# A feed-forward layer with quantised activations: one slot more in seven products, fewer quantisation passes, a head by 256 tokens

## The chip, the cores and the metric

The kernel runs on one core of one Trainium2 chip. The metric is the device time of one execution in microseconds (us). The engines are named as in the profile: PE (TensorE, matrix multiplication), DVE (VectorE), ACT (ScalarE), POOL (GpSimd) and SP (SyncE, which here only issues transfers). PE accumulates in PSUM banks; everything else lies in SBUF, the on-chip memory.

## What is computed

There are 4 batches of 1024 tokens with 512 features, a hidden width of 2048 and a condition of 128 numbers per batch.

```python
scale = cond @ norm_w.T + 1.0
ms = jnp.mean(x * x, axis=-1, keepdims=True)
h = x * (scale[:, None, :] * jax.lax.rsqrt(ms + EPS))
u = h @ up_w.T                              # 512 -> 2 * 2048
val, gate = jnp.split(u, 2, axis=-1)
h = val * jax.nn.gelu(gate, approximate=False)
hq = act_quant(h)      # per token: round(h * 127 / max|h|), then back
wq = weight_quant(down_w)   # ternary, one scale, mean|w|
y = hq @ wq.T + x
```

## The kernel before

**Tiling.** A batch is two halves of 512 tokens (`TOK`). The hidden width is 16 blocks `j` of 128 gate rows and 128 value rows. One block of one batch is a *slot* `g = b * 16 + j`. The float32 weights and activations are split into a high and a low float16 part, so that a product of two blocks needs six terms of two k-blocks each (`TERMS`).

**Plain slots and seven products.** In the first batch the slots `j < SEVEN` are plain: for each half, gate and value, 12 matmuls of 128x128 weights and 512 tokens (`plain_half`), 48 per slot. All other slots use a Strassen-Winograd form (`slot`): seven products of 6 matmuls (`product`), 42 per slot, on sums of weights and of tokens. The banks A, B and E collect them. Product 0 goes to A and is copied to B by ACT; product 4 goes to E and is copied to `v`; product 5 adds to A, and `first_value` keeps A for the second half's gate; product 1 adds to B, product 3 and 2 belong to the slot before, product 6 adds to A again, which gives the second half's value.

**Weights.** The first batch loads each block, scales it by a power of two, turns it (on PE through PSUM, or by a transposing transfer, `w_rows`), splits it and forms the sums. It spills them to DRAM; the later batches reload them through SP's queue (`s_load_x`, `s_load_y`; L909 transposing, L911 plain).

**Quantisation.** The largest |h| of each token is collected over pairs of slots (`pair_max`: a reduction L1275 and a merge L1277), spread by POOL over the partitions, and `token_scale` makes factors (L1296) and reciprocals of whole 128x128 tiles (L1302). `quant_scale` multiplies h (L1334); rounding adds and subtracts a large number, either in one DVE pass (`quant_round`, L1338) or in two ACT passes (`quant_up` L1342, `quant_down` L1346).

**Down.** The second matrix product of a batch is done one batch later, for 128 tokens `a` of both halves at a time, either plain (`down_mm`) or as a *pair* (`Pair`): seven products of 8 matmuls of 256 columns. The pairs of the last but one batch stand partly at the end, followed by the last batch's plain products.

**Order.** The code records its instructions, and a planner in the kernel (`Plan`, with costs and due times) sets the order of each engine's instructions. Each engine runs its own list strictly in that order and waits by semaphores.

**The head.** The condition gives the factors `scT` (products L690, power of two L706 to L738; for the other batches a 1536 wide multiplication L701 and sum L702). The first 512 tokens are loaded, squared and summed (L1480, L1482), scaled (L1487, L1489), turned by PE (L1494) and split into high and low parts (L1498, L1502). The first gate block is reduced (L786), scaled (L817), turned (L825) and split (L850, L859). Then PE multiplies (`plain_first`, L1199). Until then `keep_warm` gives PE matmuls without a use (L1510).

## Time and profile before

| what | before |
|---|---|
| median of 3 runs | 719.77 us (719.28 to 720.15) |
| span of the profiled execution | 717.4 us, so 2.4 us to the median lie around the span |
| PE busy | 711.5 us, 99% of the span |
| DVE busy | 605.2 us, 84% |
| ACT busy | 409.8 us, 57% |
| POOL busy | 130.0 us, 18% |
| first product | 14.36 us |
| transfers | 118.74 MB, 166 GB/s |

The span runs from the first to the last instruction on the core. A row of the timeline has start, length, engine, line, operation, out<-in and shape; what stands in brackets is the engine's idle time before it and what ended it. A row of the groups has the busy time of all instructions of a line and shape, the mean in ns, and the idle time before them. Matmuls are pipelined: one of 512 columns is given 0.379 us, while the next may start long before it ends. Engines that are not the bottleneck may be idle at no cost.

### The profile page before, as it was taken

How to read it: one execution, taken by the hardware profiler on the slowest of the kernel's cores; microseconds unless marked ns; L12 is line 12 of the kernel's file. 1: busy time of each engine (PE TensorE's matmuls, PEld its weight loads, DVE VectorE, ACT ScalarE, POOL GpSimd, SP SyncE). 2: the span in 40 equal slices, each digit the busy share in tenths (PEclk: the TensorE clock that was granted, in tenths of full speed). 3: DMA queues.
4: the chain of work that ended last, by engine and by line, in shares of the span. 5: the costliest groups of instructions: out<-in, count | busy, mean ns of one | idle time of the engine just before them, and what ended most of it. 6: DMA issues, size and time to landing. Idle time of an engine off the chain costs nothing.

```text
span 717.4 us, 10113 instructions
## 1 busy us (share of the span) xinstructions
PE 711.5 (99%) x3625; PEld 355.8 (50%) x3625; DVE 605.2 (84%) x903; ACT 409.8 (57%) x671; POOL 130.0 (18%) x138
## 2 busy tenths in 40 slices
PE   8999999999999999999999999999999999999998
PEld 4544444444444456664444445665444444445744
DVE  7978998899899899878899887767878888956897
ACT  5677688784546897553435786533333775332454
POOL 4753141020100004660023003700011000000000
PEclk9999999999999999999999999999999999999999
DMA  7778999999785896759234555778233444453414
GB/s 261 253 205 208 240 227 252 194 257 268 219 227 133 210 245 173 223 153 211 67 101 110 118 129 142 176 191 173 73 118 103 102 102 99 99 98 104 150 57 146
DMA packets 189134, 118.74 MB, mean 166 GB/s; under 512 B 151302, under 2 KB 158359, under 8 KB 189084
## 3 DMA queue, kind: packets, MB, share of 16 engines
q1 hardware_dynamic: 188794, 117.77, 64.3%
q8 instruction: 28, 0.46, 0.3%
q10 hardware_dynamic: 290, 0.33, 0.1%
q14 instruction: 22, 0.18, 0.1%
HBM read 59.20 MB, written 23.09 MB: 115 GB/s over the span
## 4 chain that ended last, share of the span: by engine, by line
PE 97%; DMA 1%; ACT 1%; POOL 0%; DVE 0%; issue 0%; SPq 0%; POOLq 0%
PE A L1141 40%; PE E L1141 20%; PE B L1141 10%; PE po L1413 9%; PE E L1156 6%; PE A L1156 4%; PE B L1156 3%; PE po L1362 2%; PE E L1362 1%; PE A L1362 1%; DMA H<-in_x_dram 1%; PE B L1413 1%; PE B L1362 0%; PE A L1199 0%; PE po L1494 0%; PE po L825 0%
## 5 line engine op out<-in xcount | busy, mean ns | idle before, releaser
L1141 PEld LDWEIGHTS <-SXY 128*128 128x128 f16 x2184 | 213.7, 98 | 250.9
L1141 PE MATMUL A<-R,SXY 128*128 128x512 f16 x1188 | 276.3, 379 | 0.0
L1141 PE MATMUL E<-R,SXY 128*128 128x512 f16 x594 | 145.3, 379 | 0.0
L1334 DVE TENSOR_TENSOR H<-H,am 128x1024 f32<-128x1024 f32 x64 | 76.6, 1222 | 0.2
L1141 PE MATMUL B<-R,SXY 128*128 128x512 f16 x312 | 76.6, 379 | 0.0
L1275 DVE TENSOR_REDUCE gm<-H 128x512 f32<-128x1024 f32 x56 | 69.0, 1232 | 0.9
L1252 ACT ACTIVATE t<-t,sg 128x512 f32<-128x512 f32 x55 | 39.7, 721 | 51.0 <-DVE t L1249 51.0
L1239 DVE SCALAR_TENSOR_TENSOR H<-A,sg,t 128x512 f32<-128x512 f32 x55 | 41.2, 749 | 31.9 <-PE A L1141 31.6
L1291 POOL PARTITION_ALL_REDUCE am<-R x8 | 15.5, 1934 | 288.4 <-DVE R L1277 288.4
L1236 ACT ACTIVATE t<-B,sg 128x512 f32<-128x512 f32 x55 | 37.8, 687 | 42.7 <-PE B L1141 42.6
L1227 ACT COPY B<-A 128x512 f32<-128x512 f32 x55 | 31.4, 571 | 53.3 <-PE A L1141 53.1
L1249 DVE TENSOR_TENSOR t<-E,t 128x512 f32<-128x512 f32 x55 | 37.9, 689 | 28.2 <-PE E L1141 27.7
L1413 PE MATMUL po<-wd,R 128*128 128x256 fp8e4 (+1 forms) x448 | 57.0, 275 | 0.0
L1219 ACT COPY t<-A 128x512 f32<-128x512 f32 x55 | 32.2, 585 | 43.4 <-PE A L1141 39.0
L1255 DVE TENSOR_TENSOR v<-A,v 128x512 f32<-128x512 f32 x55 | 37.9, 690 | 20.4 <-PE A L1141 19.6
L1413 PEld LDWEIGHTS <-R 128*128 128x128 bf16 (+1 forms) x480 | 47.0, 98 | 13.1
L1231 ACT COPY v<-E 128x512 f32<-128x512 f32 x55 | 32.2, 586 | 31.9 <-PE E L1141 15.6
L1342 ACT ACTIVATE H<-H 128x1024 f32<-128x1024 f32 x38 | 39.7, 1049 | 8.5 <-DVE H L1334 8.3
L1258 DVE SCALAR_TENSOR_TENSOR H<-v,sg,t 128x512 f32<-128x512 f32 x55 | 41.7, 759 | 1.7 <-ACT t L1252 1.4
L1156 PEld LDWEIGHTS <-SXY 128*128 128x128 f16 x264 | 25.8, 98 | 30.5
L1346 ACT ACTIVATE R<-H 128x1024 bf16<-128x1024 f32 x38 | 39.6, 1052 | 1.0 <-DVE H L1086 0.5
L1277 DVE TENSOR_TENSOR R<-R,gm 128x512 f32<-128x512 f32 x56 | 38.4, 686 | 0.9
(270 smaller groups left out, 919.2 us busy)
## 6 DMA issues: line engine op xcount, KB each, us to landing
SXY<-s_dram SPq DMA_DIRECT2D x57, 256.0 KB, 2.7
H<-in_L_cond_up_w_dram SPq DMA_DIRECT2D x13, 512.0 KB, 4.1
SXY<-s_dram SPq DMA_DIRECT2D x15, 384.0 KB, 3.7
xr<-in_x_dram SPq DMA_DIRECT2D x19, 256.0 KB, 2.9
out_dram<-xr SPq DMA_DIRECT2D x19, 256.0 KB, 2.1
s_dram<-SXY SPq DMA_DIRECT2D x12, 384.0 KB, 3.6
s_dram<-SXY SPq DMA_DIRECT2D x5, 896.0 KB, 6.7
H<-in_x_dram SPq DMA_DIRECT2D x8, 512.0 KB, 4.8
```

What stands on the lines that cost most here:

```text
L1141: PE.matmul(o, s[:, w, k, :], xs(l, k), start=start and n == 0, stop=stop and n == len(TERMS) - 1, skip_group_check=True,)
L1156: PE.matmul(ps, a[k // 2][:, w, k % 2, :], XP[:, l, k, h * TOK : (h + 1) * TOK], start=n == 0, stop=n == len(terms) - 1,)
L1239: DVE.scalar_tensor_tensor(h_half(g - 1, 0), prev["A"], gain(g - 1, 0), prev["t1"], ALU.mult, ALU.mult)
L1249: DVE.tensor_tensor(prev["t2"], prev["E"], prev["t2"], ALU.add)
L1252: ACT.activation(prev["t2"], prev["t2"], AF.Gelu, scale=gain(g - 1, 1))
L1258: DVE.scalar_tensor_tensor(h_half(g - 1, 1), prev["v"], gain(g - 1, 0), prev["t2"], ALU.mult, ALU.mult)
L1275: DVE.tensor_reduce(gm[0], v, AX.X, ALU.max, apply_absolute_value=True)
L1277: return [largest, lambda: DVE.tensor_tensor(m, m, gm[0], ALU.max)]
L1334: DVE.tensor_tensor(v, v, r.to_broadcast([P, 2, TOK]), ALU.mult)
L1342: ACT.activation(v, v, AF.Copy, bias=MAGIC)
L1346: ACT.activation(q, by_tile(v), AF.Copy, bias=-MAGIC)
L1413: PE.matmul(po, w[:, j], m, start=start and j == 0, stop=stop and j == n - 1, skip_group_check=True,)
```

## The change

1. `SEVEN` is 8 instead of 9: slot 8 goes by seven products.
2. The fourth pair of the last but one batch, at the end, is a `Pair` too; it was plain.
3. `Pair.first`: product B11 goes to one bank and ACT copies it to both halves of another one; before, its first matmul was 512 wide and wrote to both.
4. Block 2 is turned by a transfer (`w_rows(2)`) instead of by PE.
5. The head: the first 512 tokens are multiplied in two quarters of 256 (`plain_first`, `first_quarter`, `quarter_high`, `quarter_low`). Square sums and reciprocal roots come in two steps of 256 tokens. The first gate block is loaded ahead of x. The other batches' condition is loaded in the head, and its multiplication and sum stand there in DVE's order. `keep_warm` gives 20 matmuls instead of 23.
6. `first_value`: DVE writes `E = A + v`, and product 2 adds to it; before, ACT copied A out and DVE added it to E after product 2. The gelu reads E.
7. `quant_scale` writes int8 in place; one ACT copy makes bfloat16 of it.
8. Maxima over groups of 4 or 2 slots (`group_max`).
9. Reciprocals of the scales of the first three batches on a compact 32x32 tile (`token_rows`), by four small transfers; the last batch keeps `token_scale`.
10. Block maxima of the up weights come from ACT sums from block 3 on (was 6), two small operations go to POOL, and the sums of the first tokens' parts (`first_sums`) read PSUM.
11. The order is no longer planned in the kernel but read from a table (`ORDER`, a permutation of the recorded instructions).

```diff
-BY_SUM = 6
+BY_SUM = 3
-class Plan:
+class Book:
...
     def order(self):
-        steps = self.steps
...
+        packed = zlib.decompress(base64.b85decode("".join(ORDER)))
+        order, at = [], 0
+        for n in range(0, len(packed), 2):
+            at += int.from_bytes(packed[n : n + 2], "little", signed=True)
+            order.append(self.steps[at])
+            at += 1
...
-    SEVEN = 9
+    SEVEN = 8
...
     def plain_first(between):
...
+        parts = [(w, 0, k) for w in range(2) for k in range(NK)] + [(0, 1, k) for k in range(NK)]
+        order = [(t, q, *p) for t in (1, 0) for q in range(2) for p in parts[: 2 * NK]]
+        order += [(t, q, *p) for t in (1, 0) for q in range(2) for p in parts[2 * NK :]]
...
+            c = slice(q * TOK // 2, (q + 1) * TOK // 2)
             PE.matmul(
-                ps[t], a[:, w, k % 2, :], XP[:, l, k, :TOK],
-                start=w + l + k == 0, stop=l == 1 and k == NK - 1,
+                ps[t][:, c], a[:, w, k % 2, :], XP[:, l, k, c],
+                start=q + w + l + k == 0, stop=l == 1 and k == NK - 1,
...
         def first_value():
             product(5, g, cur["A"], False, True)
-            cur["t2"] = wpool.tile([P, TOK], F32, name=f"t2_{g}", tag="t2")
-            ACT.copy(cur["t2"], cur["A"])
+            DVE.tensor_tensor(cur["E"], cur["A"], cur["v"], ALU.add)
...
             product(2, g - 1, prev["E"], False, True)
-            DVE.tensor_tensor(prev["t2"], prev["E"], prev["t2"], ALU.add)
...
-            ACT.activation(prev["t2"], prev["t2"], AF.Gelu, scale=gain(g - 1, 1))
+            prev["t2"] = wpool.tile([P, TOK], F32, name=f"t2_{g}", tag="t2")
+            ACT.activation(prev["t2"], prev["E"], AF.Gelu, scale=gain(g - 1, 1))
...
-    def pair_max(b, i, h):
-        v = h_slots(b * NJ + 2 * i, 2)[:, :, h].rearrange("p j t -> p t j")
+    GROUPS = {0: (4, 4, 4, 2, 2), 1: (2, 4, 4, 4, 2), 2: (4, 4, 4, 2, 2), 3: (4, 2, 4, 4, 2)}
+    def group_max(b, j, h):
+        n = group_ends(b)[j]
+        v = h_slots(b * NJ + j - n + 1, n)[:, :, h].rearrange("p j t -> p t j")
...
+    def token_rows(b, am):
+        rows = sm.tile([NR, 2 * TOK // NR], F32, name=f"rows_{b}", tag="rows", bufs=1)
+        SP.dma_start(out=row_dram[b : b + 1], in_=am[0:1])
+        SP.dma_start(out=rows, in_=row_dram[b : b + 1].rearrange("o (r t) -> (o r) t", r=NR))
+        def invert():
+            DVE.tensor_scalar(rows, rows, 1e-5, 1.0 / 127.0, ALU.max, ALU.mult)
+            DVE.reciprocal(rows, rows)
+            SP.dma_start(out=am_dram[b : b + 1].rearrange("o (r t) -> (o r) t", r=NR), in_=rows)
+            SP.dma_start(out=am, in_=am_dram[b].partition_broadcast(P))
...
+    def whole(v):
+        return v.bitcast(I8)[:, :, :TOK]
     def quant_scale(b, i, h, s):
-        DVE.tensor_tensor(v, v, r.to_broadcast([P, 2, TOK]), ALU.mult)
+        DVE.tensor_tensor(whole(v), v, r.to_broadcast([P, 2, TOK]), ALU.mult)
-    def quant_round(b, i, h):
-        DVE.tensor_scalar(q, by_tile(v), MAGIC, MAGIC, ALU.add, ALU.subtract)
-    def quant_up(b, i, h):
-        ACT.activation(v, v, AF.Copy, bias=MAGIC)
-    def quant_down(b, i, h):
-        ACT.activation(q, by_tile(v), AF.Copy, bias=-MAGIC)
+    def quant_round(b, i, h, eng):
+        if eng is ACT:
+            ACT.copy(q, by_tile(whole(v)))
...
         def first(self, banks):
-            self.product(self.part(0, 0), "B11", k1, 1, True, True, True)
-            ACT.copy(k1[:, :HALF], k1[:, HALF:])
             self.product(self.s[1], "T1", k3, 0, True, True)
+            self.product(self.part(0, 0), "B11", k3, 1, True, True)
+            o = k3[:, HALF:].rearrange("p (y o) -> p y o", y=1).to_broadcast([P, 2, HALF])
+            ACT.copy(k1.rearrange("p (y o) -> p y o", y=2), o)
...
     first_load(0, 2)
+    w_load(0, (1,))
     first_load(2, 2)
-    w_load(0, (1,))
...
-    keep_warm(13)
-    first_sum(1)
+    keep_warm(WARM)            # WARM = 10
+    first_sum(1, DVE)
+    rsqrt(ssq0[:, 0:2], rs0[:, 0:2])
...
     def third_slot():
-        w_turn(2)
-        w_high(2)
-        w_low(2)
+        w_rows(2)
...
-    BY_VECTOR = {(0, 0), (0, 1), (1, 0), (4, 0), (6, 0), (7, 0), (7, 1)}
+    BY_VECTOR = set()
...
-    old = [pairs[a] for a in range(3)]
+    old = [pairs[a] for a in range(3)] + [Pair(b - 1, 3)]
```

**What the order does, place 1: DVE in the head.** In each row stand the line, the operation and its out<-in with the shape. `ssq` are the square sums of x, `wam` the largest values of a weight block, `rs` the reciprocal roots, `scT` the condition's factors, and the CAST makes the high part of the first gate block. Before, these rows lead to that CAST:

```order
L1482 SCALAR_TENSOR_TENSOR R,ssq_0_87<-H 128x512
L786 TENSOR_REDUCE wam_95<-H 128x1
L659 TENSOR_SCALAR wam_95<-wam_95 128x1
L793 TENSOR_SCALAR sw<-wam_95 128x1
L1489 TENSOR_SCALAR H<-H,rs_0_88 128x512
L796 RECIPROCAL iv_96<-sw 128x1
L786 TENSOR_REDUCE wam_102<-H 128x1
L659 TENSOR_SCALAR wam_102<-wam_102 128x1
L793 TENSOR_SCALAR sw<-wam_102 128x1
L737 TENSOR_SCALAR scT<-scT,ux 128x4
L796 RECIPROCAL iv_96<-sw 128x1
L850 CAST SXY<-E_100 128x2x256
```

Now the stretch from the first gate block's reduction begins with these rows, and another stretch follows with the wide reductions of blocks 1 and 2:

```order
L443 TENSOR_REDUCE wam_96<-H 128x1
L364 TENSOR_SCALAR scT<-scT 128x4
L359 TENSOR_TENSOR R<-R 128x1536
L1151 SCALAR_TENSOR_TENSOR R,ssq_0_88<-H 128x512
L366 TENSOR_REDUCE mx_92<-scT 128x1
L360 TENSOR_REDUCE scT<-R 128x3x4
L318 TENSOR_SCALAR wam_96<-wam_96 128x1
L1158 TENSOR_SCALAR H<-H,rs_0_89 128x512
L450 TENSOR_SCALAR sw<-wam_96 128x1
L1151 SCALAR_TENSOR_TENSOR R,ssq_0_88<-H 128x512
```

```order
L1158 TENSOR_SCALAR H<-H,rs_0_89 128x512
L450 TENSOR_SCALAR sw<-wam_103 128x1
L318 TENSOR_SCALAR d_0_94<-d_0_94 1x1
L453 RECIPROCAL iv_97<-sw 128x1
L383 TENSOR_SCALAR dg_95<-ident,d_0_94 1x1
L443 TENSOR_REDUCE wam_96<-H 128x2
L393 RECIPROCAL ux<-B_91 128x1
L396 COPY dx<-B_91 128x1
L395 TENSOR_SCALAR scT<-scT,ux 128x4
L443 TENSOR_REDUCE wam_103<-H 128x2
L505 CAST SXY<-E_101 128x2x256
```

The 1536 wide multiplication and sum and both wide block reductions have moved ahead of the CAST.

**Place 2: PE at the first product.** The turned blocks go to banks `po`, `A` and `E`, and the products to `B` and `A`. Before:

```order
L1494 MATMUL A_91<-ident,H 128x128
L825 MATMUL E_101<-ident,H 128x128
L1494 MATMUL A_91<-ident,H 128x128
L825 MATMUL E_101<-ident,H 128x128 x3
L1199 LDWEIGHTS SXY
L1199 MATMUL B_90<-R,SXY 128x512
```

And now, with a matmul of `keep_warm` (L1200) ahead of the first product:

```order
L1170 MATMUL po_100<-ident,H 128x128
L1170 MATMUL A_93<-ident,H 128x128
L1200 LDWEIGHTS H
L1200 MATMUL A_90<-H 128x512
L845 LDWEIGHTS SXY
L845 MATMUL B_91<-R,SXY 128x256
```

The first product now has 256 columns; all turning of the first tokens still stands ahead of it.

**Place 3: SP at the start of the second batch.** `SXY<-s_dram` are the reloads of spilled weights; `am` holds the scales on all partitions. Before:

```order
L909 DMA_TRANSPOSE SXY<-s_dram 128x4x128
L909 DMA_TRANSPOSE SXY<-s_dram 128x12x128
L945 DMA xn_111<-in_L_cond_down_w_dram 128x1024
L1310 DMA am_dram<-am_116 1x1024
L911 DMA SXY<-s_dram 128x1024
L911 DMA SXY<-s_dram 128x512
L945 DMA xt_112<-in_L_cond_down_w_dram 128x1024
```

And now:

```order
L975 DMA am_dram<-rows_127 32x32
L564 DMA_TRANSPOSE SXY<-s_dram 128x4x128
L564 DMA_TRANSPOSE SXY<-s_dram 128x12x128
L564 DMA_TRANSPOSE SXY<-s_dram 128x4x128
L976 DMA am_116<-am_dram 128x1024
L566 DMA SXY<-s_dram 128x512
L598 DMA xn_112<-in_L_cond_down_w_dram 128x1024
```

The write of the reciprocals and their broadcast now stand between reloads, and each must wait for what it moves.

696 lines of the change are left out of this document (217 added, 479 removed), and 14 rows, old and new, of tables (MENDS, MOVES).

## The prediction

> **What bounds the kernel now.** I read the share of each engine and the chain of waits first.
>
> ```profile
> span 717.4 us, 10113 instructions
> PE 711.5 (99%) x3625; PEld 355.8 (50%) x3625; DVE 605.2 (84%) x903; ACT 409.8 (57%) x671; POOL 130.0 (18%) x138
> PE 97%; DMA 1%; ACT 1%; POOL 0%; DVE 0%; issue 0%; SPq 0%; POOLq 0%
> ```
>
> TensorE (PE) is busy for 711.5 of 717.4 us and is 97% of the chain. Which part could shrink is seen in the busy time by stage (length, then busy PE, PE weight load, DVE, ACT, POOL, the granted clock, DMA share, GB/s):
>
> ```profile
> 0.00:14.36 14.36, 11.60 (x52) 5.86 (x53) 10.01 (x49) 6.20 (x13) 5.34 (x12) 1.00 0.77 247
> 14.36:20.64 6.28, 6.23 (x32) 3.14 (x32) 5.76 (x13) 5.66 (x15) 5.57 (x7) 1.00 0.95 327
> 60.00:714.40 654.40, 654.32 (x3348) 327.43 (x3346) 555.36 (x767) 369.09 (x592) 96.19 (x93) 1.00 0.64 160
> 714.40:717.40 3.00, 0.00 (x0) 0.00 (x0) 0.44 (x1) 0.00 (x0) 0.00 (x0) 1.00 0.44 152
> ```
>
> From 60 us to the end PE rests 0.08 us in 654. So the time is three things: a head until the first product at 14.36 us, PE's own work, and a 3 us tail. Work taken from DVE or ACT is worth nothing by itself there; a PE instruction taken out is worth its pitch, and a later first product costs what it is late. The pitches come from the timeline (start, length):
>
> ```profile
> 1.26 1.46 PE L1510 MATMUL A<-H 128*128 128x512 f16 x3 [1.26 <-DVE H L607]
> 3.37 2.31 PE L1510 MATMUL A<-H 128*128 128x512 f16 x5
> 5.69 0.65 PE L1510 MATMUL A<-H 128*128 128x512 f16 x2
> 7.17 2.98 PE L1510 MATMUL A<-H 128*128 128x512 f16 x13
> 18.25 1.04 PE L825 MATMUL po<-ident,H 128*128 128x128 f32 x8
> 20.64 2.75 PE L1156 MATMUL A<-R,SXY 128*128 128x512 f16 x12
> 660.18 1.04 PE L1413 MATMUL po<-wd,R 128*128 128x256 fp8e4 x8
> ```
>
> One matmul of 512 columns lasts 0.379, so twelve in 2.75 are (2.75-0.38)/11 = 0.216 apart. Eight of 256 columns, or eight float transposes, are (1.04-0.27)/7 = 0.109 apart.
>
> **The change on PE**, counted in the order of both kernels:
> - Slot 8 in seven products: 48 to 42 matmuls of 512, -6 x 0.216 = -1.30.
> - The fourth old pair as a Strassen pair: 32 x 512 becomes 56 x 256, 56 x 0.109 - 32 x 0.216 = -0.81.
> - `Pair.first` no longer sends B11 to two banks: one 512 becomes a 256 in eleven pairs, -11 x 0.107 = -1.18. ACT copies 512 columns instead of 256 there; a copy of 512 is 0.585 long (first row of the next fence), and ACT is free 43% of the span.
> - Block 2 turned by DMA: 8 transposes fewer, -8 x 0.109 = -0.87. SP gets one transposing transfer more.
> - One matmul more that sets a bank, +0.22; the head's 24 x 512 as 48 x 256, +0.05.
>
> Sum -3.89 us. That is the gain, if PE never waits where it did not wait before.
>
> **The change on DVE and ACT**, by the groups (busy us, mean ns, idle time before):
>
> ```profile
> L1219 ACT COPY t<-A 128x512 f32<-128x512 f32 x55 | 32.2, 585 | 43.4 <-PE A L1141 39.0
> L1255 DVE TENSOR_TENSOR v<-A,v 128x512 f32<-128x512 f32 x55 | 37.9, 690 | 20.4 <-PE A L1141 19.6
> L1277 DVE TENSOR_TENSOR R<-R,gm 128x512 f32<-128x512 f32 x56 | 38.4, 686 | 0.9
> L1302 DVE RECIPROCAL am<-am 128x128 f32<-128x128 f32 x32 | 27.9, 918 | 0.2
> L1334 DVE TENSOR_TENSOR H<-H,am 128x1024 f32<-128x1024 f32 x64 | 76.6, 1222 | 0.2
> L1338 DVE TENSOR_SCALAR R<-H 128x1024 bf16<-128x1024 f32 x26 | 18.0, 701 | 0.2
> L1342 ACT ACTIVATE H<-H 128x1024 f32<-128x1024 f32 x38 | 39.7, 1049 | 8.5 <-DVE H L1334 8.3
> ```
>
> DVE loses 26 roundings (18.0), 24 merges of maxima (24 x 0.686 = 16.5) and 24 reciprocals (24 x 0.918 = 22.0), some 56 us; ACT loses the 55 copies (32.2), and its 76 rounding passes become 64 (12 x 1.05 = 12.6). On the path all this is 0: PE waits for neither after 60 us. The price of a multiply that writes int8 is in no row: between 0.70 (the rounding's, with a narrow output) and twice 1.22. I take 1.22, its row now; even 64 x 1.22 = 78 us more would be 22 over the 56 saved, and the 16% that DVE is free are 112 us. The cover is gone only if a long instruction stands just ahead of one that PE needs. That place exists: `E = A + v` now stands on DVE between product 5 and product 6, which overwrites A; before, an ACT copy stood there. Product 2's six matmuls cover 1.30 us. The result needs 0.379-0.216 = 0.16 to arrive and the addition 0.69, so 0.44 is left. At worst a doubled maximum (about 2 x 1.23) has just started and PE waits 2 us; from nothing to 1.3 us over 55 slots, I take 0.2, near the lower end, since DVE stood idle 20 us before L1255 in the same position. The four small transfers of the compact scales stand on SP; they are a rival below.
>
> **The head** decides the rest.
>
> ```profile
> 6.03 0.63 ACT L1480 ACTIVATE H<-H 128x512 f32<-128x512 f32 x1 [3.25 <-DMA H<-in_x_dram]
> 7.76 0.69 DVE L1482 SCALAR_TENSOR_TENSOR R<-H 128x512 f32<-128x512 f32 x1 [0.26 <-DMA H<-in_x_dram]
> 8.42 0.69 DVE L786 TENSOR_REDUCE wam<-H 128x1 f32<-128x512 f32 x1
> 9.14 0.15 DVE L659 TENSOR_SCALAR wam<-wam 128x1 int32<-128x1 int32 x1
> 10.14 0.49 DVE L1489 TENSOR_SCALAR H<-H,rs 128x512 f32<-128x512 f32 x1 [0.66 <-POOL rs L1002]
> 10.54 0.16 DVE L796 RECIPROCAL iv<-sw 128x1 f32<-128x1 f32 x1
> 12.61 0.69 DVE L850 CAST SXY<-E 128x512 f16<-128x512 f32 x1 [0.67 <-PE E L825]
> 13.94 1.21 DVE L786 TENSOR_REDUCE wam<-H 128x2 f32<-128x1024 f32 x1
> 14.36 2.10 PE L1199 MATMUL B<-R,SXY 128*128 128x512 f16 x9 [0.37 <-ACT R L1498]
> 30.32 2.28 DVE L701 TENSOR_TENSOR R<-R 128x1536 f32<-128x1536 f32 x1
> 33.84 1.74 DVE L702 TENSOR_REDUCE scT<-R 128x12 f32<-128x1536 f32 x1
> ```
>
> The first x rows land at 6.0; the first product reads the gate weights that the CAST at 12.61 writes. In the order of the changed kernel DVE does far more before that CAST: the multiplication and sum of the other batches' scales, which now stand at 30 and 34 us, and the 1024 wide reductions of blocks 1 and 2, of which one now starts at 13.94. From DVE's first square sum (it waits for the first x rows) to the end of the CAST I count: two square sums 1.38, two scalings 0.98, one 512 wide reduction 0.69, the 1536 wide one 1.74, two 1024 wide ones 2.42, the CAST 0.69, fifteen small ones of some 0.15 = 2.25; together 10.15. Successive ones start some 0.08 before the last has ended (10.14+0.49 against 10.54), so nine long ones take 0.7 off: 9.4 us. The first gate block (256 KB) now goes ahead of x, and 192 KB of scales beside it: at 247 GB/s (the first window) 1.0 and up to 0.8 us, so x lands at 7.0 to 7.8. The CAST ends at 16.4 to 17.2. The first product then starts at 16.7 to 17.7, allowing up to 0.5 us for waits between; I take 17.2, 2.84 us later than now. That PE starts on 256 tokens instead of 512 helps only its other condition, the ACT pass at 14.36.
>
> Behind it, from 14.36 to 20.64 there are 24 x 0.216 + 8 x 0.109 = 6.05 us of PE work in 6.28, so 0.23 of waiting. Changed, the low gate part comes one 256 wide and one 512 wide DVE instruction behind the CAST (0.4, an estimate from half of 0.69, and 0.69), and six products of 0.109 cover 0.65 of that: 0.4 of waiting; the value weights' low parts come behind it in the same way, another 0.4. I take 0.8, with 0.3 and 1.6 (twice that) as ends. That is +0.57.
>
> Sum: -3.89 + 2.84 + 0.57 + 0.20 = -0.28 us. The span becomes 717.1. The median of the runs is 719.77, the profiled span 717.4, so 2.4 us lie around it: **719.5 us**. Its own range, from 16.7, 0.3 and 0 to 17.7, 1.6 and 1.3, is 718.3 to 721.9, most of it below 721.2. 0.2% of this time, about what the runs can tell from no change, is 1.44 us.
>
> [...] PE stands nearly idle for about 3 us ahead of that CAST, with fewer keep-warm matmuls (20, not 23). In the rows above, the matmuls at 3.37 are (2.31-0.38)/4 = 0.48 apart (0.43 in pairs) and those at 7.17 0.217, with the granted clock given as 1.00: PE was slow from its first matmul at 1.26 until between 5.69 and 7.17. If that state returned, it would last 4.4 to 5.9 us of products and cost half of it, 2.2 to 3.0 us.
> [...]
>
> **The rivals.**
> 1. *Faster: the head is not later.* DVE may reach the CAST as early as now if the long reductions run while it would wait for x anyway, and 256 tokens need half the turned columns. Then -3.89 + 0.2 + 0.2 = -3.5, 716.3 us. For it: DVE waits before 6.0 and 0.66 at 10.14. Against: 9.4 us of instructions behind x do not fit between 6.0 and 13.3. Chance 0.21, the cases between included.
> 2. *Slower: reloads just in time.* Each batch reloads spilled weights through SP's queue. They land (min, median, max us) in
>
> ```profile
> DMA to landing us min/median/max: 2.6/3.9/6.7
> DMA to landing us min/median/max: 2.2/2.8/5.9
> ```
>
> for the transposing ones (L909) and the plain ones (L911). In the changed order SP has, among them at each batch's start, the transfers of the scales, of which the broadcast waits for DVE's reciprocal, and some reloads stand only 18 to 28 matmuls (3.9 to 6.0 us) ahead of their first product. A landing of 6.7 then holds PE up by 0.7 to 2.8 us. Against: the median is below. From one such wait per later batch (3 x 0.7 = 2.1) it decides: 721.2 to 724, say 722. Chance 0.13.
> 3. *Slower: the slow clock*, as above: 719.5 + 2.6 = 722.1. Against: turning matmuls fall into the gap. Chance 0.10.
> 4. That the change does not do what it says would show in PE's count; the order excludes it.
>
> **How the numbers follow.** My forecast has 0.56, within 0.2% by its own range. Rival 1 gives faster 0.21; rivals 2 and 3 slower 0.23. About 0.1 of rival 1 lies below 717.0, and about 0.1 of the slower cases above 722.3, so that is the range.
>
> **What would show it.** Right: the CAST of the first gate block ends near 17 us, the first product (L845) starts at 16.7 to 17.7, PE's work is 3.9 us less, and no PE wait behind 25 us; DVE falls to some 550 us with no effect. Wrong: a first product before 15.5 (rival 1), PE waits for DMA at batch starts (2), pitches of 0.218 for 256 columns in the head (3), or PE waits for `E = A + v` summing to over 1.3 us.

## The result, and the profile after

The changed kernel takes 740.36 us (median of 4 runs) against 719.63 of the kernel before beside it, a ratio of 1.0283 [1.0263, 1.0303]: 2.8% slower, where 719.5 was forecast. The profiled execution has a span of 737.9 us, 20.5 more than before. The first lines of its page and the shares of the chain:

```profile
span 737.9 us, 10039 instructions
PE 714.2 (97%) x3657; PEld 360.1 (49%) x3657; DVE 570.8 (77%) x789; ACT 365.4 (50%) x622; POOL 142.7 (19%) x164
PE 70%; DVE 16%; issue 4%; POOL 2%; ACT 2%; DVEq 0%; ACTq 0%; POOLq 0%
```

DVE is busy 34 us less than before and stands 167 us idle, and yet it is now 16% of the chain, where it was 0%. The stages show where (length, then busy PE, PE weight load, DVE, ACT, POOL, granted clock, DMA share, GB/s):

```profile
0.00:20.13 20.13, 13.18 (x49) 7.08 (x49) 14.46 (x53) 5.72 (x13) 6.16 (x14) 0.83 0.73 231
81.00:100.00 19.00, 14.96 (x62) 6.18 (x61) 18.24 (x29) 11.78 (x22) 4.38 (x6) 0.91 0.78 208
100.00:734.60 634.60, 625.55 (x3236) 316.15 (x3233) 489.25 (x613) 296.70 (x486) 88.70 (x95) 1.00 0.61 155
```

From 100 us on PE rests 9 us in 635, between 81 and 100 another 4 (before, from 60 us on: 0.08 in 654). What PE waited for, summed by the instruction that ended the wait (us in total, times, longest):

```profile
PE E L802 <- DVE H L830: 3.7, 2, 3.0
PE A L787 <- DVE E L865: 3.6, 6, 0.9
PE A L373 <- DVE mx L366: 3.5, 1, 3.5
PE A L787 <- DVE v L901: 2.9, 4, 1.0
PE E L787 <- DVE E L865: 1.4, 2, 0.8
PE A L787 <- DVE H L885: 0.8, 1, 0.8
```

Nearly every wait behind the head is for DVE, at four different instructions (`E = A + v` is L865), none for a transfer. DVE's groups (busy us, mean ns, idle before) tell what is dear and what is not:

```profile
L1010 DVE TENSOR_TENSOR H<-H,am 128x1024 int8<-128x1024 f32 x64 | 76.4, 1224 | 0.9 <-DMA am<-am_dram 0.7
L932 DVE TENSOR_REDUCE gm<-H 128x512 f32<-128x2048 f32 x18 | 66.9, 3718 | 0.0
L927 DVE TENSOR_REDUCE R<-H 128x512 f32<-128x2048 f32 x6 | 22.3, 3716 | 0.0
L932 DVE TENSOR_REDUCE gm<-H 128x512 f32<-128x1024 f32 x14 | 17.2, 1231 | 0.2
```

The int8 multiply costs what the float32 one did (1.224). The maximum over 4 slots, 24 times, costs 3.72 us: three times that over 2 slots (1.23), not twice. One of the waits, in the timelines of DVE and of PE:

```profile
130.41 3.69 DVE L932 TENSOR_REDUCE gm<-H 128x512 f32<-128x2048 f32 x1
134.01 0.68 DVE L901 TENSOR_TENSOR v<-A,v 128x512 f32<-128x512 f32 x1
134.74 1.45 PE L787 MATMUL A<-wd,SXY 128*128 128x512 f16 x6 [0.95 <-DVE v L901]
```

The reduction waits for nobody; behind it stands the addition that must read bank A before PE may overwrite it. The five rows for L787 and L802 above are 15 waits; in 13 of them a 3.7 us reduction lies in the 5 us ahead.

The rest is in the head. DVE's rows:

```profile
7.77 1.75 DVE L359 TENSOR_TENSOR R<-R 128x1536 f32<-128x1536 f32 x1
9.44 0.68 DVE L1151 SCALAR_TENSOR_TENSOR R<-H 128x512 f32<-128x512 f32 x1
10.05 0.15 DVE L366 TENSOR_REDUCE mx<-scT 128x1 f32<-128x4 f32 x1
10.12 1.74 DVE L360 TENSOR_REDUCE scT<-R 128x12 f32<-128x1536 f32 x1
18.14 0.17 DVE L393 RECIPROCAL ux<-B 128x1 f32<-128x1 f32 x1 [2.02 <-PE B L389]
19.62 0.67 DVE L505 CAST SXY<-E 128x512 f16<-128x512 f32 x1
```

and those of ACT (the first x rows land) and PE (the power of two of the scale; keep-warm; the first product):

```profile
8.46 0.63 ACT L1149 ACTIVATE H<-H 128x512 f32<-128x512 f32 x1 [5.68 <-DMA H<-in_x_dram]
10.26 0.27 PE L373 MATMUL A<-ident,mx 128*1 128x128 f32 x1 [3.45 <-DVE mx L366]
14.78 1.91 PE L1200 MATMUL A<-H 128*128 128x512 f16 x4
20.35 0.50 PE L845 MATMUL B<-R,SXY 128*128 128x256 f16 x3 [0.19 <-DVE SXY L505]
```

x lands at 8.46 (6.03 before), DVE turns to it at 9.44, behind a 1536 wide multiplication, and the first product comes at 20.35 instead of 14.36. Behind the wait of 3.45 PE is slow: four matmuls in 1.91 are (1.91-0.63)/3 = 0.427 apart.

For the accounts I take the starts of all matmuls from the trace. The time from the first product to the last matmul is split into waits (what a matmul starts later than the usual distance of its kind, over 0.02 us) and work (the rest); behind the last matmul comes the tail. Before: 14.36 + 0.61 + 699.08 + 3.40 = 717.4. After: 20.35 + 18.83 + 695.24 + 3.51 = 737.9. So the head costs 6.0, the waits 18.2, the work is 3.84 less.

### The profile page after: what moved, and what is told of

It reads as the page before. It is cut to its first block, busy times and chain, and to the rows that moved or that the text cites. A ratio compares the mean times of both kernels' runs of the same rounds, so it can differ in the third digit from the quotient of the medians.

```text
span 737.9 us, 10039 instructions
## 1 busy us (share of the span) xinstructions
PE 714.2 (97%) x3657; PEld 360.1 (49%) x3657; DVE 570.8 (77%) x789; ACT 365.4 (50%) x622; POOL 142.7 (19%) x164
## 4 chain that ended last, share of the span: by engine, by line
PE 70%; DVE 16%; issue 4%; POOL 2%; ACT 2%; DVEq 0%; ACTq 0%; POOLq 0%
PE A L787 33%; PE E L787 16%; PE B L787 7%; PE po L1083 7%; DVE gm L932 5%; PE po L1033 2%; PE E L802 2%; DVE R L927 1%; DVE E L865 1%; DVE H L885 1%; PE E L1033 1%; DVE v L901 1%; PE B L1083 1%; PE A L1033 1%; DVE H L904 1%
## 5 line engine op out<-in xcount | busy, mean ns | idle before, releaser
L787 PEld LDWEIGHTS <-SXY 128*128 128x128 f16 x2184 | 213.6, 98 | 250.3 <-issue 11.3
L787 PE MATMUL A<-R,SXY 128*128 128x512 f16 x1188 | 290.3, 379 | 5.8 <-DVE E L865 3.0
L787 PE MATMUL E<-R,SXY 128*128 128x512 f16 x594 | 153.1, 379 | 0.8 <-DVE E L865 0.8
L932 DVE TENSOR_REDUCE gm<-H 128x512 f32<-128x2048 f32 (+1 forms) x32 | 84.1, 2630 | 0.3
L787 PE MATMUL B<-R,SXY 128*128 128x512 f16 x312 | 83.1, 379 | 0.0
L885 DVE SCALAR_TENSOR_TENSOR H<-A,sg,t 128x512 f32<-128x512 f32 x56 | 41.9, 748 | 48.1 <-PE A L787 39.1
L1010 DVE TENSOR_TENSOR H<-H,am 128x1024 int8<-128x1024 f32 x64 | 76.4, 1224 | 0.9 <-DMA am<-am_dram 0.7
L898 ACT ACTIVATE t<-E,sg 128x512 f32<-128x512 f32 x56 | 38.4, 688 | 71.7 <-PE E L787 71.7
L1015 ACT CAST R<-H 128x1024 bf16<-128x1024 int8 x64 | 65.4, 1044 | 15.3 <-DVE H L1010 14.7
L1083 PE MATMUL po<-wd,R 128*128 128x256 fp8e4 x448 | 66.1, 273 | 0.2 <-DVE R L1071 0.2
L901 DVE TENSOR_TENSOR v<-A,v 128x512 f32<-128x512 f32 x56 | 38.5, 688 | 27.8 <-PE A L787 27.7
L865 DVE TENSOR_TENSOR E<-A,v 128x512 f32<-128x512 f32 x56 | 39.0, 697 | 26.9 <-PE A L787 20.2
L802 PEld LDWEIGHTS <-SXY 128*128 128x128 f16 x264 | 26.1, 99 | 34.5 <-issue 6.0
L802 PE MATMUL E<-R,SXY 128*128 128x512 f16 x132 | 32.7, 392 | 3.0 <-DVE H L830 3.0
L1124 DVE SCALAR_TENSOR_TENSOR xr<-po,dq,xr 128x256 f32<-128x256 f32 (+1 forms) x36 | 21.4, 611 | 9.7 <-PE po L1083 6.6
```

The source lines that it names most:

```text
L787: PE.matmul(o, s[:, w, k, :], xs(l, k), start=start and n == 0, stop=stop and n == len(TERMS) - 1, skip_group_check=True,)
L802: PE.matmul(ps, a[k // 2][:, w, k % 2, :], XP[:, l, k, h * TOK : (h + 1) * TOK], start=n == 0, stop=n == len(terms) - 1,)
L865: DVE.tensor_tensor(cur["E"], cur["A"], cur["v"], ALU.add)
L885: DVE.scalar_tensor_tensor(h_half(g - 1, 0), prev["A"], gain(g - 1, 0), prev["t1"], ALU.mult, ALU.mult)
L898: ACT.activation(prev["t2"], prev["E"], AF.Gelu, scale=gain(g - 1, 1))
L901: DVE.tensor_tensor(cur["v"], cur["A"], cur["v"], ALU.add)
```

## Experiments

All runs stand in one table. e14 and e16 start from the kernel before, all others from the changed one. The columns are time and ratio to the kernel before (its medians were 719.4 to 719.7), start of the first product, waits behind it, and PE's work, in us.

| run | time | ratio | first product | waits | work |
|---|---|---|---|---|---|
| before | 719.63 | 1 | 14.36 | 0.61 | 699.08 |
| after | 740.36 | 1.0283 [1.0263, 1.0303] | 20.35 | 18.83 | 695.24 |
| e1_half | 722.62 | 1.0044 [1.0029, 1.0058] | 20.44 | 1.56 | 695.30 |
| e2_split | 742.23 | 1.0324 [1.0309, 1.0340] | 20.43 | 23.44 | 695.26 |
| e3_head | 746.98 | 1.0376 [1.0360, 1.0392] | 20.38 | 23.81 | 695.20 |
| e4_headsplit | 748.95 | 1.0406 [1.0391, 1.0422] | 19.76 | 28.50 | 695.21 |
| e5_twice | 722.04 | 1.0036 [1.0024, 1.0049] | 19.74 | 1.86 | 695.28 |
| e6_condhalf | 726.54 | 1.0101 [1.0086, 1.0116] | 18.32 | 7.23 | 695.26 |
| e7_head2half | 726.63 | 1.0098 [1.0083, 1.0113] | 16.21 | 10.01 | 695.24 |
| e8_forms | 728.13 | one run | 19.04 | 8.52 | 695.26 |
| e9_threes | 731.95 | 1.0173 [1.0158, 1.0188] | 19.52 | 11.07 | 695.28 |
| e10_head3threes | 738.43 | 1.0262 [1.0215, 1.0308] | 16.10 | 21.35 | 695.23 |
| e11_xfirst | 724.28 | 1.0067 [1.0052, 1.0082] | 22.57 | 1.35 | 695.28 |
| e12_scalefirst | 721.74 | 1.0033 [1.0021, 1.0045] | 19.99 | 1.91 | 695.26 |
| e13_scalewide | 724.74 | 1.0084 [1.0064, 1.0103] | 19.75 | 4.53 | 695.25 |
| e14_first | 727.19 | 1.0106 [1.0092, 1.0119] | 14.89 | 9.39 | 697.87 |
| e15_nocond | 722.55 | 1.0036 [1.0022, 1.0049] | 21.33 | 2.14 | 695.28 |
| e16_firstk2 | 724.71 | 1.0074 [1.0061, 1.0087] | 14.53 | 7.10 | 697.88 |
| e17_headnocond | 721.73 | 1.0037 [1.0024, 1.0051] | 16.25 | 4.89 | 695.25 |

### The maxima: is it their price?

e1 reduces only the last two slots of each group of four, in the same places.

```diff
-        v = h_slots(b * NJ + j - n + 1, n)[:, :, h].rearrange("p j t -> p t j")
+        v = h_slots(b * NJ + j - 1, 2)[:, :, h].rearrange("p j t -> p t j")
```

> The changed kernel, but each group of 4 slots takes its maximum over its last two slots only, so that the other two are left out of the scale; order and number of instructions stay, and the 24 reductions of 3.7 us become 1.23. Theory M (the 18 us of PE waits behind the first product come from these long reductions in DVE's strict order): the waits behind the first product fall from 18.5 to 3 us or less, 740.4 becomes 724 +- 3. Rival Q (the order is too tight whatever the reductions last, because E = A + v and the other additions now stand on DVE between two products): the waits stay above 12 us, at least 735.

The time falls to 722.62, the waits from 18.8 to 1.6, the head stays. So the long reductions make the waits. Whether two slots less or the price of four is what counts, e1 does not tell.

e5 reduces all four slots in two instructions of two, one right behind the other (the second overwrites the first, so one half of the maxima is lost): 2.46 us instead of 3.72 in each place.

```diff
+        v = [h_slots(b * NJ + k, 2)[:, :, h].rearrange("p j t -> p t j") for k in range(j - n + 1, j, 2)]
...
-            DVE.tensor_reduce(out, v, AX.X, ALU.max, apply_absolute_value=True)
+            for w in v:
+                DVE.tensor_reduce(out, w, AX.X, ALU.max, apply_absolute_value=True)
```

> The changed kernel, but the reduction over 4 slots is given as two reductions over 2 slots one behind the other (1.23 each, so 2.46 instead of 3.7); the first pair's result is written over, so two slots of each group are left out of the maximum. Theory M2 (the order fits reductions that cost twice a pair's, and only the excess of 1.24 us, 24 times, makes DVE late): the waits behind the first product fall to 1 to 4 us, 722.6 (as halved) to 727. Rival M3 (any instruction or group of instructions of over 2 us at those places holds PE up): the waits stay at 8 us or more, 731 or more.

722.04 us. The reductions in the groups of this run:

```profile
L931 DVE TENSOR_REDUCE gm<-H 128x512 f32<-128x1024 f32 x50 | 61.6, 1232 | 0.9
```

The waits (us in total, times, longest):

```profile
PE A L374 <- DVE mx L367: 3.5, 1, 3.5
...
PE A L788 <- DVE v L902: 0.4, 1, 0.4
```

With 2.46 in each place the order of the changed kernel has next to no waits, although `E = A + v`, the int8 multiply and the four small transfers of the scales are all still in it. The excess, 24 x (3.72 - 2.46) = 30 us of an engine that is idle 167, costs PE 17 us. A place in a fixed order has a size, and the instruction is larger than the place.

The first product is 0.6 us earlier here (19.74 instead of 20.35) for another reason: behind the same wait of 3.5 the same four keep-warm matmuls took 1.34 us instead of 1.91, and the float transposes are back at 0.27 each from 16.02 us on, in the changed kernel (0.42 until 16.9) from 17.52. A first product that moves by 0.6 us between two runs is therefore no proof that one order is better.

```profile
14.84 1.34 PE L1207 MATMUL A<-H 128*128 128x512 f16 x4
```

e2 goes back to pairs of slots with a merge each, and puts the first pair's reduction and merge behind the end of an earlier slot (the diff is in words).

```diff
-            largest over 4 slots, then one merge, at the old place
+            largest over slots 1 and 2 and its merge, behind the slot's last L904
+            largest over slots 3 and 4, at the old place; its merge as before
```

> The changed kernel, but a group of 4 is taken as two pairs again: the first pair's reduction (1.23) and merge (0.69) stand behind the instruction that ends the slot in which they became ready, the second pair's where the long reduction stood (the first group of a batch: both in one place). DVE has as much work as with pairs everywhere. Theory M: like the halved one or up to 3 us slower, 724 to 728. Rival Q: 735 or more. A third, that only DVE's total counts: DVE's busy time falls by some 13 us, and the time by as much in proportion to the long reductions, to about 733.

It missed theory M: 742.23, with 23.4 of waits. The time lies in rival Q's range, but Q (too tight whatever the reductions last) is what e1 and e5 exclude. The reductions are short here, and DVE is busy less than in the changed kernel:

```profile
L941 DVE TENSOR_REDUCE gm<-H 128x512 f32<-128x1024 f32 x56 | 68.9, 1231 | 0.5
```

and yet PE's waits are

```profile
PE A L794 <- DVE v L911: 5.2, 4, 1.6
PE po L1118 <- DVE xr L1159: 3.7, 2, 2.3
```

So DVE's sum does not decide either: a reduction and a merge (1.23 + 0.69 = 1.92 us) in new places, beside 1.23 in the old ones, make more waits than the long reductions did (18.8), while 2.46 in the old places alone made next to none.

e8 takes four kinds of long reduction in turn, all with 512 results: four slots, three slots, both halves of two slots, and four neighbouring elements.

```diff
+            if k % 4 == 1:   # three slots
+                v = h_slots(b * NJ + j - 2, 3)[:, :, h].rearrange("p j t -> p t j")
+            elif k % 4 == 2: # four inputs, 2048 bytes apart
+                v = two.rearrange("p j h t -> p t (j h)")
+            elif k % 4 == 3: # four inputs, 4 bytes apart
+                v = two.rearrange("p j h t -> p (j h t)").rearrange("p (t j) -> p t j", j=4)
```

> The changed kernel with four kinds of the long reduction in turn, each 512 outputs, which leaves slots out of the maximum or takes others: 4 slots (stride 4096 bytes), 3 slots (4096), 4 half slots (stride 2048), 4 neighbours (stride 4). Theory S (the stride of 4096 costs): 3.7, 2.8, 3.7 or 2.4, 2.4 us. Theory N (a fixed price for each output beside the elements, pairs at 1.23 us): 4 inputs cost under 2.46 everywhere, so it falls if the neighbours take 3.7 as well. Theory W (four inputs cost more than two pairs whatever the stride): 3.7, 2.5 to 2.8, 3.7, 3.7.

Its timeline, in the order both halves of two slots, four neighbours, three slots, and an ordinary pair of slots:

```profile
111.47 3.77 DVE L941 TENSOR_REDUCE gm<-H 128x512 f32<-128x2048 f32 x1
127.08 2.27 DVE L941 TENSOR_REDUCE gm<-H 128x512 f32<-128x2048 f32 x1
165.17 1.89 DVE L941 TENSOR_REDUCE gm<-H 128x512 f32<-128x1536 f32 x1
172.26 1.23 DVE L941 TENSOR_REDUCE gm<-H 128x512 f32<-128x1024 f32 x1
```

Per input these are 1.84, 1.11, 1.23 and 1.20 ns. The halves of two slots cost what four slots do: the twelve reductions of these two kinds take 3.72 in the mean (44.8 + 13.4 us for 18 of 2048 inputs, less six neighbours at 2.27), the longest of L941 3.77. So the step is between three and four inputs that lie far apart (4096 or 2048 bytes); four neighbours stay at 1.11 ns. Neither the stride alone nor the number alone does it; why four far inputs do is open.

e9 uses that: sets of three slots (1.90) where they fit, two pairs with a merge in the ten other places.

```diff
+    TAKES = {0: {3: (0, 4), 7: (4, 3), 11: (7, 3), 13: (10, 3), 15: (13, 3)}, ...}
```

> The whole computation of the changed kernel in its order, but the maxima are taken over other sets at the same places: mostly 3 slots in one reduction (1.90 us by the run with four kinds), and where 4 remain (10 of the 40 reductions) two of 2 slots with a merge between (1.23 + 0.69 + 1.23). No reduction of 3.7 us is left. Theory M2: waits behind the first product of 1.5 to 5 us, 722 to 726. Rival M3 (at the places where two pairs and a merge, 3.15 us, stand, PE waits as with 3.7): 10 x 1 us, 729 to 733.

It missed theory M2's range upwards, 731.95: 11 us of waits are left. The time lies in rival M3's range, but not by its mechanism: there are not ten waits of 1 us. One place gives 4.5 of the 11, a wait of 2.92 that ends at 94.84 and 1.4 of slow matmuls behind it: the first three take 1.44, where 0.216 apart they take 0.81 (in the changed kernel the wait of 2.96 there is followed by 19 in 5.67, 1.40 over the usual 4.27). From 81 us on two reductions and a merge (1.22 + 1.22 + 0.69) stand there ahead of a crowded stretch of DVE:

```profile
PE E L803 <- DVE H L831: 3.3, 2, 2.9
```

(PE's waits above, the timeline of DVE and of PE below)

```profile
91.89 2.23 DVE L702 TENSOR_TENSOR xt<-am 128x256 f32<-128x256 f32 x1
94.84 1.44 PE L803 MATMUL E<-R,SXY 128*128 128x512 f16 x3 [2.92 <-DVE H L831]
```

### The head: which of its chains?

The next runs move steps of the head in the changed kernel's table; each diff names what stands earlier (+) or later (-) than in it. "Waits" below are PE's.

e3: the largest scale and the power of two early, the multiplication of the other batches' condition directly ahead of them, the wide reductions of blocks 1 and 2 later, six keep-warm matmuls more.

```diff
+ DVE L366 mx, PE L373, DVE L379 to L383, PE L389 (with L359 ahead)
- DVE L443 (1024 wide, blocks 1 and 2), L360
```

> The changed kernel with its long reductions, but another order in the head: the largest scale and its power of two ahead of the wide multiplication, the first gate block's path ahead of the wide reductions, and six keep-warm matmuls more. Theory H (the head is late because DVE's order holds back the largest scale and the first CAST): the first product starts at 14.5 to 16 instead of 20.35, PE has no 3.5 us wait and no cold stretch, the time falls by 4.5 to 6 us to 734 to 736. Rival L (the head is late because x lands late, behind the first gate block): the first product stays behind 18 us, and the time falls by 2 us at most.

Worse than both theories had it, 746.98, with the first product where it was (20.38) and new waits of 1.8 and 1.5 for DVE behind it. The multiplication then waits for its own transfer, and PE, which waits for the power of two behind it, with it:

```profile
7.18 1.76 DVE L367 TENSOR_TENSOR R<-R 128x1536 f32<-128x1536 f32 x1 [1.73 <-DMA R<-in_cond_dram]
```

(the timeline above, PE's waits below)

```profile
PE B L397 <- DVE dx L404: 5.0, 1, 5.0
```

e4 has the edits of e2 and e3 together. Expected were 718 to 723 if both gains add up, and 730 or more by rival Q; it took 748.95, the slowest of all runs. Neither edit was a gain by itself, and together they were none: of its 28.5 us of waits, 5.2 are for `v` and 3.7 in the down products, as in e2, and ahead of the first product PE waits 4.4 us for the power of two, much as in e3.

e6: half maxima as in e1, and the load of the other batches' condition with its two 1536 wide instructions behind the first products.

```diff
- ACT L338 load of the other batches' condition; DVE L359, L360; PE L402
```

> The halved maxima (two slots of each group left out), and in the head alone the other batches' condition put back: its load, which 128 partitions read from one row, is issued behind the first products, its multiplication and sum stand behind them on DVE. Against the halved kernel, 722.6, whose first product starts at 20.4 us. Theory C (that load slows all others, the bytes landed per half microsecond fall from 135 KB to 30 to 90 between 3 and 5.5 us, and its 3.5 us of DVE work hold up the largest scale): x lands 1 to 2 us sooner, the largest scale is done at 7 to 8.5 instead of 10.1, the first product starts at 16 to 18, the time is 718 to 720.5. Rival P (what holds the first product is PE's slow clock and the chain behind x): 20 +- 0.7, the time 722 to 723.

Both theories missed. x lands no sooner (8.60) and the first product comes at 18.32, two us earlier than in e1; but PE then waits 3.4 us for the turning of the condition, and the total is 4 us above that of e1.

e7: in addition the largest scale and the first gate block ahead on DVE, POOL and PE, and eight keep-warm matmuls more.

```diff
+ DVE L366, PE L373, DVE L379 to L396; DVE L443 (first block), POOL L472, PE L480
- DVE L443 (blocks 1 and 2)
```

> As the last, and besides the largest scale's chain ahead of all else, the first gate block's path ahead of the second's on DVE, POOL and PE, and eight keep-warm matmuls more. Theory H: the first product starts at 13.5 to 15.5, no stretch at the slow clock behind 10 us, the time is 715.5 to 718, faster than the kernel before by the PE work that the change saves (3.9) less 0 to 2. Rival P: not before 17, 719 or more.

The first product is at 16.21, four us earlier than in e1 and the changed kernel, though not at theory H's 13.5 to 15.5. The time is that of e6, 726.63, and far from H's 715.5 to 718. The largest wait:

```profile
PE po L410 <- DVE scT L372: 3.4, 1, 3.4
```

and the place in PE's timeline:

```profile
30.28 0.38 PE L410 MATMUL po<-ident,scT 128*16 128x128 f32 x1 [3.39 <-DVE scT L372]
```

The 3.5 us of 1536 wide work, taken out of the head, come back as one wait of 3.39 that begins at 26.9 us. The run's mean granted clock is 0.995, that of e17, where this wait is 0.29, is 0.999; the 2.5 us of slow clock behind it that the expectation of e17 takes off is the author's estimate.

e10 (e9 with x loaded first, the condition's load later and its turning behind the second half's) and e11 (e5 with x loaded ahead of the first gate block, nothing else):

```diff
+ SP L1136 load of the first x rows, ahead of SP L434
- e10 only: ACT L338, DVE L359 and L360, PE L402 and the row's store
```

> As the last, and the head in another order: x ahead of the first gate block, the largest scale's chain ahead of all else on DVE and PE, the first gate block ahead of the second on DVE, POOL and PE, eight keep-warm matmuls more, the other batches' condition loaded behind the first products, its DVE work spread behind them and its transposition moved behind the second half's turning. Theory H (order and loads make the head): first product at 14 to 15.5, no stretch at the slow clock, 5 to 6 us less than without: 716.5 to 720.5. Rival: the wait goes to the condition or to the low parts again, as in the two runs before (3.5 us): 721 to 724.

> The kernel with two reductions of 2 slots in the place of each over 4 (722.0, first product at 19.7), and only one thing besides: x's first load is issued ahead of the first gate block's. Theory L (a part of the head is the load order): x lands at 6 to 6.7 instead of 8.4, the first product starts 1 to 2 us sooner, 720 to 721. Rival D (DVE's order alone: it waits for the gate block's maximum ahead of x's square sum): nothing gained, or up to 1 us lost, 721.7 to 723.

Both missed. In e11 x lands at 7.95 instead of 8.52, but the gate block later; DVE's order has the block's reduction first, so all comes 2.8 us later. In e10 x lands at 5.42: only both loads out of its way bring it early. Its first product (16.10) is that of e7, and 21 us of waits lie behind it; the largest new ones are 2.9 for DVE at 41 us and 2.0 for a transfer at 59 us.

e12 is e5 with the largest scale and the power of two right behind the condition's sums, and nothing else but keep-warm. It tries the wait of 3.45 alone.

```diff
+ DVE L366, PE L373, DVE L379, L380, L318, L383, PE L389 (ahead of DVE L443)
+ PE L1200 x8 behind them
```

> The changed kernel with each long maximum as two short reductions (as in the twice run, 722.04), and in the head only this moved: the largest condition scale, its way through PE and the power of two stand right behind the sums of the condition, ahead of the first gate block's reduction; 8 keep-warm matmuls more behind it. Theory S (PE's wait of 3.5 us for the largest scale, and the going to and fro of the power of two between DVE and PE behind it, make the head late): DVE saves its idle time of 0.99 and five small instructions of 0.86 in all, so the first product comes at 17.9 instead of 19.7, the clock is full from 7 us on, and the time is 720.2 (719.5 to 720.8). Rival B (what bounds the head is the sum of DVE's work up to some 28 us, in whatever order): the first product is earlier, but PE waits as much more behind it: 721.5 to 722.5. Rival P (POOL's scaling of the gate block at 15 us and the turning on PE behind it set the first product, not DVE): first product at 19 or later, 721.3 to 722.

721.74, which the intervals do not tell from e5 (722.04). The wait is gone, and another is in its place:

```profile
PE po L1184 <- ACT H L1170: 2.7, 1, 2.7
```

What that ACT pass waits for is seen in the timelines of DVE and POOL:

```profile
10.43 0.68 DVE L1165 SCALAR_TENSOR_TENSOR R<-H 128x512 f32<-128x512 f32 x1
15.93 1.38 POOL L480 TENSOR_SCALAR H<-H,iv 128x512 f32<-128x512 f32 x2 [0.89 <-DVE iv L461]
19.25 0.69 DVE L513 CAST SXY<-E 128x512 f16<-128x512 f32 x1 [1.17 <-PE E L488]
```

x's square sum stands on DVE behind the 1536 wide multiplication; from it the way goes over POOL's roots, the scaling and the turning, and POOL scales the gate block only behind the roots of the second 256 tokens. DVE now waits 1.17 at the CAST for PE. The first product (19.99) and the time are those of theory P, not of S.

e13 moves DVE's two wide reductions behind the block's parts as well.

```diff
- DVE L443 (1024 wide, blocks 1 and 2)
```

> The run before, and DVE's two 1024 wide reductions of blocks 1 and 2 (2.4 us) stand behind the first gate block's high and low parts instead of ahead of them. Theory S with the short chain: first product at 16.5 to 17.3 (2.4 us less of DVE work ahead, with the turned block as the next limit), and 0.5 us more of waits behind it: 719.0 to 719.8. Rival B (sum of DVE's work): first product at 16.5 to 17.3, but 1 to 2 us of waits behind it up to 30 us, so no faster than the run before, 720 to 721.5.

Both theories missed: no earlier product (19.75), 2.6 us more of waits behind it than in e12, and 724.74.

e15 is e5 with the 1536 wide pair cut to 96, in its places, which leaves out 120 of the condition's 128 terms; e17 is e7's head with that cut and e5's maxima.

```diff
+        e = slice(0, 8)
-        DVE.tensor_tensor(v, w, s, ALU.mult)
+        DVE.tensor_tensor(v[..., e], w[..., e], s[..., e], ALU.mult)
```

> The changed kernel with each long maximum as two short reductions (twice run, 722.04); left out are 120 of the 128 terms in the other batches' scale (their multiplication and sum are 96 wide instead of 1536, 0.2 us each instead of 1.75, in the same places of DVE's order and with the same transfer ahead), so the outputs of three batches are wrong. Theory W (the two 1536 wide instructions, 3.5 us, stand on the way from the first x rows to the first product: the first square sum of DVE waits behind the one, the second behind the other): first product at 16.7 to 17.2 instead of 19.7, and the time 718.5 to 719.3. Rival P (the way over POOL's roots and scalings and the turning takes as long by itself): first product at 18.5 or later, 720.5 to 722.

> The head of the run e7_head2half (largest scale and power of two first, the first gate block ahead on DVE, POOL and PE, wide reductions of blocks 1 and 2 behind it, 8 keep-warm matmuls more, the other batches' condition behind the first products) with each long maximum as two short reductions, and, as in e15_nocond, 8 of the 128 terms in the other batches' scale, so that its two instructions are 96 wide instead of 1536. Theory F (the first product comes when DVE, POOL and PE are all reordered, and what e7 gave back at 26.6 us was the 3.5 us of these two instructions): first product at 16.2, PE's waits behind it 10.0 - 3.6 - 2.5 (slow clock behind that wait) = 3 to 4.5 us, work 695.3: time 717.5 to 719.3, the first below the kernel before. Rival G (other work of the first 35 us takes the place of these two on DVE, since DVE is busy nearly all the time there): waits behind the first product 6 to 9 us and 720.5 to 723.

e15, 722.55, is no faster than e5, and its first product (21.33) is later, as rival P allows and theory W does not. In its profiled execution (the longest of five, 724.06; the shortest was 720.81) the square sums were done at 9.3, but POOL's first instruction started at 10.99 though the profile shows nothing it waited for ("issue"):

```profile
10.99 0.18 POOL L653 TENSOR_SCALAR ssq<-ssq 128x2 f32<-128x2 f32 x1 [10.56 <-issue]
```

So e15 does not settle its theory W. In e17 the product comes at 16.25, as F said; its waits are 4.9, just above F's 3 to 4.5, and 721.73 lies in G's range. F's own terms do not give the range that stands there: with the tail (3.5) and the 1.8 us by which this run's time exceeds its span they add up to 719.8 to 721.3. (The 2.4 us ahead of the prediction set a median against the span of another execution; within one execution it is 1.7 to 1.8 in the runs here.) So e17 speaks for F by its product and its waits, and the total, 0.4 above, decides little. First product and waits together are 21.1 there, 21.6 in e5, 22.0 in e1, 21.9 in e12, 23.5 in e15 and 24 to 26 in e6, e7, e11 and e13; before, they are 15.0. No order tried got the head back.

### PE's work by itself

e14 is the kernel before in its own order, with the 256 wide B11 and the wide copy of the new `Pair.first` alone. One thing stays as before: T1 stands behind B11, while the changed kernel has it ahead of B11.

```diff
-            self.product(self.part(0, 0), "B11", k1, 1, True, True, True)
-            ACT.copy(k1[:, :HALF], k1[:, HALF:])
+            self.product(self.part(0, 0), "B11", k3, 1, True, True)
+            ACT.copy(k1 (both halves), k3[:, HALF:])
```

> The kernel before, in its own order instruction by instruction, with one part of the change alone: the pair's first product goes to one half of a bank, 256 wide, and ACT copies it to both halves of another bank (eleven pairs). If the PE term of the prediction holds, eleven matmuls become 0.107 us shorter each: PE busy 1.2 us less, span 716.2 instead of 717.4, time 718.3 (718.0 to 718.6). Rival: the copy, which is 512 wide instead of 256, comes too late for the product behind it in the same bank; then PE waits up to 0.3 us in each of eleven places and the time is 719 to 722.

PE's work falls by 1.21 us (1.18 expected), and the time rises to 727.19, by the rival's mechanism at more than twice its price (0.66 in a place, where up to 0.3 was expected):

```profile
PE po L1496 <- ACT po L1504: 6.3, 10, 0.7
```

One of these ten places, ACT and PE (an eleventh, at bank E, waits 0.7 as well):

```profile
281.67 0.57 ACT L1504 COPY po<-po 128x512 f32<-128x512 f32 x1 [0.20 <-PE po L1496]
282.29 0.81 PE L1496 MATMUL po<-wd,H 128*128 128x256 fp8e4 x6 [0.66 <-ACT po L1504]
```

The next product, T1, stops behind two matmuls until the copy, which reads the other half of its bank, has ended. e16 puts B11 into the second bank instead (`k2` for `k3` in both new lines; the pairs' sums come out other in it, so only its time is read).

> The kernel before in its own order, with the pair's first product in one half of the second bank, 256 wide, and the ACT copy to both halves of the first bank; the product T1, eight matmuls of 0.109, goes to a third bank and does not wait for the copy (in the run e14_first it shared the bank that the copy read, and PE waited 0.66 us in each of eleven places). PE term: busy 1.2 us less, span 716.2, time 718.2 (717.9 to 718.6). Rival: the copy of 0.57 us and the ways there and back (some 0.2 each) take longer than the 0.87 of T1, so PE waits 0.1 to 0.3 in each of eleven places: 719.3 to 721.5.

Again both were missed, 724.71. The wait moves and does not go: in six of the eleven places that bank is still being read by the pair before.

```profile
PE po L1496 <- DVE xr L1536: 5.5, 6, 1.0
```

The work is 1.20 less again. In the changed kernel the term comes without such a wait: T1 is already done when the copy reads the bank, and behind B11 its order has products of the slots.

## Why the prediction was wrong

- **PE's work, -3.89: right.** It is -3.84, and -3.78 to -3.88 in every run with the changed PE program; the one part tried alone gave -1.21 for -1.18.
- **DVE, "On the path all this is 0": the step that failed, by 17 us.** The prediction priced a maximum over 4 slots as "a doubled maximum (about 2 x 1.23)" and never bounded that from a row; it is 3.72. It then argued with DVE's idle sum (112 us). The order, however, is fixed, and the question in each place is what stands behind the long instruction and whether PE waits for it. e5 shows that 2.46 would have done no harm: the mechanism ("The cover is gone only if a long instruction stands just ahead of one that PE needs") was named, with `E = A + v` as its place and 1.3 us as its upper end; 5.0 us came there, and 7.4 at places of the same kind, `v` (L901) and the products with the gate (L885, and L830 of the plain slots). Of the other 6 of the 18, 1.4 are the slow clock behind the wait of 2.96 and 2.4 what these 15 waits leave out (they count from the end of the matmul before, 0.16 behind the usual distance); the rest are short waits.
- **The int8 price: right**, 1.224 for 1.22. DVE fell to 570.8 instead of 550: the long reductions added 30 us that the sum did not have, and some 9 fell in smaller items that it did not count.
- **The first product, +2.84: it is +6.0.** By the forecast's own steps the CAST ends at 7.4 + 9.4 = 16.8; it ended at 20.29. x landed at 8.46, 1.06 later than the middle of 7.0 to 7.8; DVE came to it 0.98 later still, since the 1536 wide multiplication stood ahead of the square sum; DVE's work from there was 8.83 instead of 9.4; and 2.02 went into waiting for PE, for which up to 0.5 had been allowed. The forecast followed DVE alone and added what it does; in the trace the chain goes to PE and POOL and back. e12 and e13 show that taking away one of these alone does not bring the product forward; which share each has stays open.
- **Waits right behind the first product: right in size.** 0.8 was taken, the distances there give 0.7.
- **The rivals.** Reloads just in time did not come: no wait of PE for a transfer has a row. The faster head did not come. The slow clock did: after 3.45 us of waiting in the head, with a granted clock of 0.83 up to 20 us, and after 2.96 at 93 us (0.91 from 81 to 100 us). Behind the first, which ends at 10.26, PE needed some 7 us to be back (transposes of 0.42 until 16.9, of 0.27 from 17.52); the second cost 1.4 us (19 matmuls in 5.67, which 0.216 apart take 4.27; the granted clock is 0.58 from 96 to 100 us). In e12 a wait of 2.73 stands ahead, as the profile counts it, and four keep-warm matmuls took 1.91 again. In e7 no wait of PE between 7 and 17 us is over 1.48, and it kept its full rate there (nine keep-warm matmuls in 2.12, 0.217 apart); in e17 the transposes from 15.16 us on take 0.27. Neither became faster than the kernel before. So the slow clock in the head does not explain the total by itself.
- **The side.** The slower rivals had 0.23 in all, each of 2 to 3 us; none was a price of DVE's, though the change's largest new instruction had no row in the trace.

## What to carry to other kernels

An instruction that no trace has shown is bounded from below and above before it is put into a fixed order, even on an engine with a quarter of its time free: what counts is the wait behind it in its place, and 1.26 us too much in 24 places cost 17 us. A start that goes over four engines is followed along what each waits for, not by one engine's sum of work; in e6 and e7 the 3.5 us of DVE's work that were moved out of it came back as a wait of 3.4. A gain in PE's work is only seen when both are in order: here -3.8 us were there in every run of the changed kernel and never in the time.

## What the runs showed of the hardware that was not expected

- A maximum over four inputs that lie 2048 or 4096 bytes apart takes 3.7 us for 512 results, over three 1.90, over two 1.23, over four neighbours 2.27. Two and three far inputs pay next to nothing against neighbours (1.20 and 1.23 ns per input against 1.11), four pay 1.84. What makes the step no run shows.
- Where the first gate block or the other batches' condition is loaded beside it, the first x rows land at 7.95 to 8.6; with both behind them (e10) at 5.42. The condition's 192 KB are one row spread over 128 partitions, and moving it alone (e6: 8.60) or the block alone (e11: 7.95) gains little against the 8.46 of the changed kernel.
- POOL's first instruction on the square sums started 1.7 us behind their end in e15 (10.99 against 9.29), where the profile shows nothing that it waited for, and 0.2 to 0.6 behind it in e17 (9.20 against 9.03) and e10 (9.33 against 8.69); that is as much as one of the steps above. It was not followed further.
